# Transposing normalised rows with VectorE block turns and transfers through memory, in a planned transformer kernel on one core

## The chip, the core and the metric

The kernel runs on one core of a Trainium2 chip. The core has five engines with their own instruction queues: PE (TensorE, matrix products), DVE (VectorE), ACT (ScalarE), POOL (GpSimd) and SP (SyncE, which here issues nearly all DMA transfers). [...] The metric is the device time of the whole program in microseconds (us); lower is better.

## What is computed

Four attention blocks follow one another on a tensor of 8 batches x 256 rows x 128 features, all in float32. Block L2 is by far the largest: six layers, each with self-attention (16 heads of 64), cross-attention to 64 context rows, and a feed-forward part. Each of these three parts begins with a layer norm of its input. Cut to that:

```python
def _ln(x, g, b, eps=1e-05):
    m = jnp.mean(x, axis=-1, keepdims=True)
    v = jnp.mean(jnp.square(x - m), axis=-1, keepdims=True)
    return (x - m) / jnp.sqrt(v + eps) * g + b

def step(t, p):
    tn = _ln(t, norm_g, norm_b)
    t = _mha(tn, tn, skv, sq, sow, sob, tgt_mask) + t
    tn = _ln(t, norm_g, norm_b)
    t = _mha(src, tn, ckv, cq, cow, cob, src_mask) + t
    tn = _ln(t, pg, pb)
    t = t + (jax.nn.relu(tn @ w1 + b1) @ w2 + b2)
    return (t, None)
out, _ = jax.lax.scan(step, tgt, stacked)
```

Batches are independent of each other inside L2. L0 and L1 before it and L3 after it are single attention blocks.

## The kernel before

**Tiling.** One batch is 256 rows, kept as two tiles of 128 partitions by 128 features in `t`. [...] each normalised batch `xn` (rows on partitions) has to be turned into `tT` (128 features on partitions, 256 rows along the free dimension). There are 8 batches x 6 layers x 3 parts = 144 such turns.

**The helper `ahead`** (lines 764 to 816) makes each of them, in four steps with a place in the plan each: `moments` (L776, L777: mean and variance on DVE), `scales` (L782 to L789: reciprocal root and, for two of the three callers, minus mean times it, on POOL), `normal` (L795 on ACT for cross-attention and feed-forward, L800 on DVE for self-attention, writes `xn`) and `trans`. `trans` takes a PSUM tile, transposes the two 128x128 tiles of `xn` on PE against an identity (L809), and lets ACT copy the result to `tT` with the layer norm's gain and bias (L811).

**The plan.** The order of work is written by hand. `at(tick, phase, fn)` enters a function; at the end all functions are run in the order of tick, then phase, and every instruction of PE, DVE, ACT and POOL is tied behind the one before it on its engine. So the phase fixes the order on each engine inside a tick. SP is not among the tied engines.

- Self-attention of batch b at tick T = T0 + 4b: `exps` puts eight exponentials (L885) on ACT in each of ticks T to T+3, at phases 2 and 2.1, each preceded by a mask-and-minimum on DVE (L880). `scores` (L866) stand on PE at phases 1 and 1.1. The projections of the *next* batch run in the same ticks: k and q at T-4 and T-3 (L829, phases 3.5 to 3.7), v at T-2 and T-1 (L848). `values` (L921) and `out_proj` (L939) follow at phase 3 of later ticks.
- Cross-attention takes two ticks a batch: scores L341 and L348 on PE, then `lower` (copy L357 on ACT, maximum L359 on DVE, subtraction L360 on POOL), exponential L366 on ACT at phase 8, then sum L370, multiply L372 and turn L380 in the next ticks, and sums L388 on PE.
- Feed-forward takes one tick a batch: `first` (L1071 on PE, then ReLU L1076 on ACT) at T, `second` (L1088 on PE, added by L1092 on DVE) at T+1. Its last four ticks run together with the first projections of the next layer.

**Buffers and transfers.** PSUM has four two-bank tiles, shared by all products and transposes. Weights of a layer have one buffer each, and are loaded by SP in three functions `load_sa`, `load_ca` and `load_ff`, each issued at one place in the plan. SP also loads a mask of four transfers a batch (L246).

Of the kernel before, what the change touches and what calls it, by code (L numbers as in the profile page):

```python
# [8 lines left out]
F32 = mybir.dt.float32  # L9
I32 = mybir.dt.int32  # L10
BF16 = mybir.dt.bfloat16
AF = mybir.ActivationFunctionType
# [4 lines left out]
P = 128  # L17
B, S, D = 8, 256, 128
# [4 lines left out]
QT = S // P  # L23
# [4 lines left out]
def tile_xattn_stack(ctx: ExitStack, tc: tile.TileContext, io, out: bass.AP):  # L28
    nc = tc.nc
# [11 lines left out]
    def uniq(base):  # L41
        counter[0] += 1
        return f"{base}_{counter[0]}"
# [7 lines left out]
    def tp_tile():  # L51
        return one_bank("tp")
# [8 lines left out]
    def sb(shape, tag, bufs=2, pool=None):  # L61
        return (pool or act).tile(shape, F32, tag=tag, name=uniq(tag), bufs=bufs)
# [46 lines left out]
    ident = const.tile([P, P], F32, tag="ident", name="ident")  # L109
# [85 lines left out]
    def load_sa(l):  # L195
        sk = sb([D, H * HD], "w_sk", 1, wpool)
        nc.sync.dma_start(out=sk, in_=io["L2_sa_kv"][l][:, : H * HD])

        sv = sb([D, 4, 2, 2 * HD], "w_sv", 1, wpool)
        sv_v = io["L2_sa_kv"][l][:, H * HD :].rearrange("p (g a x) -> p a g x", g=2, a=4)  # L200
        for a in range(4):
            nc.sync.dma_start(out=sv[:, a], in_=sv_v[:, a])
        sq = sb([D, H * HD], "w_sq", 1, wpool)
        nc.sync.dma_start(out=sq, in_=io["L2_sa_q"][l])
        sow = sb([P, HC, D], "w_sow", 1, wpool)
        nc.sync.dma_start(out=sow, in_=io["L2_sa_ow"][l].rearrange("(c p) d -> p c d", p=P))
        ob = sb([P, D], "w_sob", 1, wpool)
        nc.sync.dma_start(out=ob, in_=io["L2_sa_ob"][l].partition_broadcast(P))
        W["sa", l] = (sk, sv, sq, sow, ob)

    def load_ca(l):

        ckv = sb([P, H * HD], "w_ckv", 1, wpool)
        for i in range(2):
            nc.sync.dma_start(
                out=ckv[DM * i : DM * i + DM],
                in_=io["L2_ca_kv"][l][:, H * HD * i : H * HD * (i + 1)],
            )
        cq = sb([D, H * HD], "w_cq", 1, wpool)
        nc.sync.dma_start(out=cq, in_=io["L2_ca_q"][l])  # L220
        cow = sb([P, HC, D], "w_cow", 1, wpool)
        nc.sync.dma_start(out=cow, in_=io["L2_ca_ow"][l].rearrange("(c p) d -> p c d", p=P))
        ob = sb([P, D], "w_cob", 1, wpool)
        nc.sync.dma_start(out=ob, in_=io["L2_ca_ob"][l].partition_broadcast(P))
        W["ca", l] = (ckv, cq, cow, ob)

    def load_ff(l):
        w1 = sb([D, FF], "w_f1", 1, wpool)
        nc.sync.dma_start(out=w1, in_=io["L2_ff_w1"][l])
        w2 = sb([P, FF // P, D], "w_f2", 1, wpool)  # L230
        nc.sync.dma_start(out=w2, in_=io["L2_ff_w2"][l].rearrange("(c p) d -> p c d", p=P))
        ob = sb([P, D], "w_fb", 1, wpool)
        nc.sync.dma_start(out=ob, in_=io["L2_ff_b2"][l].partition_broadcast(P))
        W["ff", l] = (w1, w2, ob)
# [44 lines left out]
    def at(tick, phase, fn):  # L279
        plan.setdefault(tick, []).append((phase, fn))  # L280
# [489 lines left out]
    def ahead(b, stats_at, normal_at, tT_at, g, bias, st, on_scalar=True):  # L770

        def moments():
            st["mv"] = sm([P, QT, 2], "mv")
            for j in range(QT):
                six = sm([P, 6], "six")
                nc.vector.bn_stats(six, tt(b)[:, j, :])  # L776
                nc.vector.bn_aggr(st["mv"][:, j, :], six)  # L777

        def scales():
            mv = st["mv"]  # L780
            ve = sm([P, QT], "ve")
            nc.gpsimd.tensor_scalar(ve, mv[:, :, 1], 1e-5, None, ALU.add)  # L782
            st["rstd"] = sm([P, QT], "rstd")
            nc.gpsimd.tensor_tensor(st["rstd"], ve, mhalf, ALU.pow)  # L784
            if on_scalar:
                nm = sm([P, QT], "nm")
                nc.gpsimd.tensor_tensor(nm, mv[:, :, 0], st["rstd"], ALU.mult)
                st["nm"] = sm([P, QT], "nm2")
                nc.gpsimd.tensor_scalar(st["nm"], nm, -1.0, None, ALU.mult)  # L789

        def normal():
            st["xn"] = sb([P, QT, D], "xn", 3)
            for j in range(QT):
                if on_scalar:
                    nc.scalar.activation(  # L795
                        st["xn"][:, j, :], tt(b)[:, j, :], AF.Identity,
                        scale=st["rstd"][:, j : j + 1], bias=st["nm"][:, j : j + 1],
                    )
                else:
                    nc.vector.tensor_scalar(  # L800
                        st["xn"][:, j, :], tt(b)[:, j, :], st["mv"][:, j, 0:1],
                        st["rstd"][:, j : j + 1], ALU.subtract, ALU.mult,
                    )

        def trans():
            ps = tp_tile()
            xn = st.pop("xn")
            for j in range(QT):
                nc.tensor.transpose(ps[:, j * P : (j + 1) * P], xn[:, j, :], ident)  # L809
            st["tT"] = sb([D, S], "tT", 3)  # L810
            nc.scalar.activation(st["tT"], ps[:, :S], AF.Identity, scale=g, bias=bias)  # L811

        at(*stats_at, moments)
        at(stats_at[0], 8.4, scales)
        at(*normal_at, normal)
        at(*tT_at, trans)

    def plan_sa(l, b, T):
# [134 lines left out]
        def mask():  # L953
            st["nm"] = load_mask(b)

        ahead(b, (T - 6, 8.3), (T - 5, 2.6), (T - 5, 7.2), norm_g, norm_b, st, False)
        at(T - 2, -1, mask)
        at(T - 4, 3.6, lambda: project(W["sa", l][2], "q", HD ** -0.5, 0, False))
        at(T - 4, 3.7, lambda: project(W["sa", l][2], "q", HD ** -0.5, 1, False))
# [58 lines left out]
    def plan_ca(l, b, T):  # L1018
        st = {}
        fold = W["fold", l]  # L1020

        def keys_both():

            res = [big("q", shape=(D, 4, 4, M)) for _ in range(2)]
            for g in range(2):
                ps = two_banks("mm").rearrange("p (r a x) -> p r a x", r=2, a=4)
                for a in range(4):
                    for r in range(2):
                        rows = slice(r * DM, (r + 1) * DM)
                        nc.tensor.matmul(  # L1030
                            ps[:, r, a, :], lhsT=fold["AT"][rows, 4 * g + a, :],
                            rhs=ctx2[rows, b : b + 2, :].rearrange("p b m -> p (b m)"),
                            start=True, stop=True,
                        )
                for i in range(2):
                    nc.scalar.copy(
                        res[i][:, :, 2 * g : 2 * g + 2, :].rearrange("p a r k -> p r a k"),
                        ps[:, :, :, i * M : (i + 1) * M],
                    )
            keys_of[b], keys_of[b + 1] = res  # L1040

        def make_values():
            st["VW"] = values_of(b, fold["WVO"])

        def res():
            st["tb"] = residual(b, W["ca", l][3])

        ahead(b, (T - 4, 6), (T - 3, 2.95), (T - 2, 2.9), norm_g, norm_b, st)
        if b % 2 == 0:
            at(T - 2, 3.7, keys_both)  # L1050
        at(T + 2, 3.2, make_values)
        at(T + 2, 7, res)

        def add(qt, ps):
            nc.vector.tensor_add(t[:, QT * b + qt, :], ps[:, :D], st["tb"][:, qt, :])

        for qt in range(QT):
            plan_weights_64(
                T + qt, qt, lambda: st["tT"], lambda: keys_of[b], lambda: st["VW"],
                nm2[:, b].unsqueeze(1).to_broadcast([P, 4, M]), lambda ps, qt=qt: add(qt, ps),  # L1060
            )

    def plan_ff(l, b, T):
        st = {}
# [28 lines left out]
                tt(b), ps[:, :S].rearrange("p (a d) -> p a d", a=QT), st["tb"]  # L1093
            )

        ahead(b, (T - 3, 6), (T - 2, 3.3), (T - 1, 2.9), pre_g[:, l : l + 1], pre_b[:, l : l + 1], st)
        at(T, 3.1, first)
        at(T + 1, 3.2, second)

# [61 lines left out]
            at(T + n, 4.5 - 0.1 * n, step)  # L1161


    at(0, -1, lambda: load_sa(0))
    at(8, -1, lambda: load_ca(0))
    at(8, -0.9, lambda: load_ff(0))
    plan_start()
    for b in range(B):
# [3 lines left out]
    for l in range(NL):  # L1172
        T_ca = T0 + 4 * B
        T_ff = T_ca + 2 * B
        for b in range(B):
            plan_sa(l, b, T0 + 4 * b)
        plan_ca_weights(l, T_ca - 6)
        for b in range(B):
            plan_ca(l, b, T_ca + 2 * b)
            plan_ff(l, b, T_ff + b)  # L1180
        if l > 0:
            at(T0, -1, lambda l=l: load_ff(l))
        if l + 1 < NL:
            at(T_ca + 4, -1, lambda l=l: load_sa(l + 1))
            at(T_ff + 1, -1, lambda l=l: load_ca(l + 1))
        T0 = T_ff + B
    def keys_l3():
        S0["k3T"] = sb([D, B, M], "AT", 1, heap)
# [3 lines left out]
    for b in range(B):  # L1192
# [1 line left out]

    engines = (
        mybir.EngineType.PE, mybir.EngineType.DVE, mybir.EngineType.Activation,
        mybir.EngineType.Pool,
    )
    order = mybir.DependencyInfo(mybir.DependencyClass.NoSync, mybir.DependencyReason.DATA)
    last = {}  # L1200
# [68 lines left out]
```

## Time and profile before

| | |
|---|---|
| median of 3 runs | 2530.57 us (2528.28 to 2533.17) |
| profiled execution, its own time | 2528.09 us |
| its span, first to last instruction | 2526.4 us |
| mean granted TensorE clock | 0.975 |
| busy: PEld (weight loads) | 1765.0 us, 70% |
| busy: DVE, ACT, POOL | 1822.0 (72%), 1735.1 (69%), 1443.0 us (57%) |
| the 288 transposes L809 on PE | 69.8 us busy, 307 ns each |
| the 144 copies L811 on ACT | 54.7 + 27.0 us busy, 570 and 563 ns each |
| DMA traffic | 64.31 MB, mean 25 GB/s |

A busy share is an average over stages. A layer takes about 380 us of the span; in the second one, for example, self-attention lies between about 570 and 800 us, cross-attention between about 800 and 900 us, and feed-forward, with the start of the next layer, up to about 957 us. PE's busy time is modelled from pipelined matmuls, so what PE costs is better read from the chain of waits and from the starts of instructions than from the busy share.

### The profile page before, as it was taken

To read this page: it belongs to the slowest core of one execution; us is meant where nothing else is said; L and a number is where in the kernel's file an instruction comes from. 1 tells how busy PE (TensorE), PEld (TensorE's weight loads), DVE (VectorE), ACT (ScalarE), POOL (GpSimd) and SP (SyncE) were. 2 spreads that over 40 slices of the span, in tenths; PEclk is the share of its full clock that TensorE was granted. 3 is DMA by queue.
4 is the path that set the end of the run, shared out by engine and by line. 5 is a ranking of instruction groups with operands and counts; after the bars stand their busy time and mean duration, and the time that the engine had idled before them with its cause. 6 is when DMAs were issued, how large, how long until landed. Compare 5 with 4: busy or idle time off the path is not lost.

```text
span 2526.4 us, 100196 instructions
## 1 busy us (share of the span) xinstructions
PE 2393.0 (95%) x42507; PEld 1765.0 (70%) x42507; DVE 1822.0 (72%) x5976; ACT 1735.1 (69%) x4537; POOL 1443.0 (57%) x2477
## 2 busy tenths in 40 slices
PE   6899999999999999999989999989999989999996
PEld 3566777776777776777776777776777776777774
DVE  3677887748887747887747887747887756888764
ACT  3467777657777657777657777657778657778651
POOL 2655556845556844555854555854555763555763
PEclk8999999999999999999999999999999999999996
DMA  5000012000002000002000102000012000000000
GB/s 161 11 2 20 19 35 64 2 8 24 20 28 65 8 7 24 20 20 70 12 2 21 28 20 70 12 2 20 20 28 70 12 2 20 20 20 12 3 1 17
DMA packets 94770, 64.31 MB, mean 25 GB/s; under 512 B 7729, under 2 KB 90353, under 8 KB 94322
## 3 DMA queue, kind: packets, MB, share of 16 engines
q1 hardware_dynamic: 93874, 57.64, 8.3%
q8 instruction: 334, 5.47, 0.9%
q14 instruction: 114, 0.93, 0.1%
q10 hardware_dynamic: 448, 0.26, 0.0%
HBM read 55.78 MB, written 2.10 MB: 23 GB/s over the span
## 4 chain that ended last, share of the span: by engine, by line
PE 69%; POOL 13%; DVE 8%; ACT 7%; issue 3%; DMA 0%; POOLq 0%; DVEq 0%; SPq 0%; ACTq 0%
PE mm L921 14%; PE mm L829 13%; PE sc L866 12%; PE mm L939 7%; PE mm L848 7%; POOL e L360 6%; PE mm L1071 3%; DVE m L359 3%; PE mm L1088 3%; POOL e L372 3%; ACT e L357 2%; PE mm L388 2%; ACT e L885 2%; PE sc L341 1%; POOL rstd L784 1%
## 5 line engine op out<-in xcount | busy, mean ns | idle before, releaser
L895 POOL TENSOR_SCALAR e<-e,rs 128x256 f32<-128x256 f32 x1536 | 702.5, 478 | 690.8 <-DVE rs L893 682.2
L885 ACT ACTIVATE e<-e,mn 128x256 f32<-128x256 f32 x1536 | 758.3, 495 | 131.0 <-DVE mn L880 130.2
L880 DVE CUSTOM_DVE_ANT_0 e<-sc,nm 128x256 f32<-128x256 f32 x1536 | 542.8, 419 | 122.5 <-PE sc L866 122.3
L905 DVE STREAM_TRANSPOSE eTc<-e 128x512 f32<-128x512 f32 x768 | 519.9, 697 | 66.2 <-POOL e L895 64.6
L921 PE MATMUL mm<-eTc,v 32*64 32x256 f32 x12288 | 381.2, 386 | 18.5 <-ACT AT L1007 8.1
L866 PE MATMUL sc<-k,q 64*32 64x256 f32 x12288 | 378.9, 380 | 5.9 <-DVE mn L880 4.2
L921 PEld LDWEIGHTS mm<-eTc,v 32*64 32x64 f32 x12288 | 284.1, 134 | 112.5 <-issue 27.7
L866 PEld LDWEIGHTS sc<-k,q 64*32 64x32 f32 x12288 | 220.2, 106 | 125.3 <-issue 45.8
L360 POOL TENSOR_TENSOR e<-e,m 128x1024 f32<-128x1024 f32 x112 | 213.1, 1903 | 148.6 <-DVE m L359 141.9
L885 ACT ACTIVATION_READ_ACCUMULATOR e<-e,mn 128x1 f32 x1536 | 286.7, 187 | 0.0
L359 DVE TENSOR_REDUCE m<-sc 128x16 f32<-128x1024 f32 x112 | 137.2, 1225 | 179.4 <-ACT e L357 179.4
L388 PE MATMUL mm<-v,k 128*128 128x128 f32 x1792 | 235.5, 287 | 5.9 <-DVE k L380 5.4
L388 PEld LDWEIGHTS mm<-v,k 128*128 128x128 f32 x1792 | 219.1, 200 | 27.4 <-issue 12.1
L341 PE MATMUL sc<-q,tT 128*32 128x256 f32 x3072 | 217.1, 382 | 0.0
L372 POOL TENSOR_TENSOR e<-e,r 128x1024 f32<-128x1024 f32 x112 | 213.2, 1904 | 0.7 <-DVE r L371 0.7
L366 ACT ACTIVATE e<-e 128x1024 f32<-128x1024 f32 x112 | 119.0, 1062 | 115.8 <-POOL e L360 115.8
L829 PE MATMUL mm<-tT,w_sk 128*128 128x256 f32 x768 | 189.6, 390 | 0.0
L286 ACT COPY v<-mm 128x1024 f32<-128x1024 f32 x96 | 97.2, 1012 | 133.1 <-PE mm L848 133.1
L939 PEld LDWEIGHTS mm<-w_sow,o 128*128 128x128 f32 x1536 | 175.1, 192 | 17.7 <-issue 14.4
L848 PE MATMUL mm<-w_sv,tT 128*32 128x256 f32 x3072 | 185.7, 382 | 0.0
L939 PE MATMUL mm<-w_sow,o 128*128 128x128 f32 x1536 | 183.6, 278 | 1.5 <-ACT WVO L1007 1.5
L829 PE MATMUL mm<-tT,w_sq 128*128 128x256 f32 x768 | 173.6, 379 | 0.0
(210 smaller groups left out, 3521.9 us busy)
## 6 DMA issues: line engine op xcount, KB each, us to landing
nm<-mask_d SPq DMA_DIRECT2D x192, 128.0 KB, 3.0
w_sk<-in_L_sa_kv_dram SPq DMA_DIRECT2D x6, 512.0 KB, 9.4
w_sv<-in_L_sa_kv_dram SPq DMA_DIRECT2D x24, 128.0 KB, 2.4
w_sq<-in_L_sa_q_dram SPq DMA_DIRECT2D x6, 512.0 KB, 3.5
w_sow<-in_L_sa_ow_dram SPq DMA_DIRECT2D x6, 512.0 KB, 4.0
w_ckv<-in_L_ca_kv_dram SPq DMA_DIRECT2D x12, 256.0 KB, 4.2
w_cq<-in_L_ca_q_dram SPq DMA_DIRECT2D x6, 512.0 KB, 4.6
w_cow<-in_L_ca_ow_dram SPq DMA_DIRECT2D x6, 512.0 KB, 4.0
```

The source lines that it names most:

```text
L360: nc.gpsimd.tensor_tensor(e, e, m.unsqueeze(2).to_broadcast([P, 16, M]), ALU.subtract)
L372: nc.gpsimd.tensor_tensor(tl["e"], tl["e"], r.unsqueeze(2).to_broadcast([P, 16, M]), ALU.mult)
L388: nc.tensor.matmul(ps[:, :D], lhsT=eT[:, s].rearrange("p q x -> p (q x)"), rhs=vw[:, r, k, g, :], start=(s == 0), stop=(s == 7),)
L829: nc.tensor.matmul(ps[:, i * S : (i + 1) * S], lhsT=w[:, c * P : (c + 1) * P], rhs=st["tT"], start=True, stop=True,)
L848: nc.tensor.matmul(ps[32 * a : 32 * a + 32, i, :], lhsT=st["tT"][:, kb * 32 : (kb + 1) * 32], rhs=sv[:, a].rearrange("p g x -> p (g x)"), ...
L866: nc.tensor.matmul(sc[32 * a : 32 * a + 32, r, j, :], lhsT=st["q"][g][rows, a, qb * 32 : (qb + 1) * 32], rhs=st["k"][g][rows, a, :], start ...
L880: nc.vector.tensor_tensor_reduce(e[:, i, :], sc4[:, i, :], st["nm"][:, 2 * jj + i % 2, :], -1.0, 3.0 * BIG, ALU.add, ALU.min, mn[:, i : i ...
L885: nc.scalar.activation(e[:, i, :], e[:, i, :], AF.Exp, scale=-1.0, bias=mn[:, i : i + 1], accum_out=rs[:, i : i + 1],)
L895: nc.gpsimd.tensor_scalar(e[:, i, :], e[:, i, :], rs[:, i : i + 1], 1.0, ALU.mult, ALU.mult)
L905: nc.vector.transpose(eT[:, r, :, 2 * jj : 2 * jj + 2, :], e[:, 2 * r : 2 * r + 2, :].rearrange("p j (k x) -> p k j x", x=32),)
L921: nc.tensor.matmul(ops[a // 2][r * HD : (r + 1) * HD, a % 2, :S], lhsT=st["v"][kb // 4][rows, kb % 4, (2 * g + r) * HD : (2 * g + r + 1) * ...
L939: nc.tensor.matmul(st["ps"][:, j * D : (j + 1) * D], lhsT=st["oT"][c // 4][:, c % 4, j * P : (j + 1) * P], rhs=sow[:, c, :], start=(c == 0 ...
```

## The change

`trans` no longer uses PE. A new step `blocks` turns each 32x32 block of `xn` on DVE into a tile `z`, and four transfers issued by SP write the blocks to a scratch tensor in memory, sorted by feature. A new step `fetch` reads them back with one transfer of 128 partitions x 1 KB into `raw`. `trans` then is only the ACT instruction with gain and bias, reading `raw` instead of PSUM. `trans` also moves to a later place in the plan for each of the three callers. SP joins the engines whose order is tied to the plan. The weight loads become generators, whose parts are entered in the plan one by one.

```diff
+        def blocks():
+            xn = st.pop("xn")
+            z = sb([P, 4, QT, 32], "z", 2)
+            nc.vector.transpose(z, xn.rearrange("p q (j x) -> p j q x", x=32))
+            zd = st["zd"] = dram.tile([4, 32, 4, QT * 32], F32, tag="zd", name=uniq("zd"), bufs=4)
+            for j in range(4):
+                nc.sync.dma_start(
+                    out=zd[j].rearrange("b i x -> i b x"), in_=z[:, j].rearrange("p q x -> p (q x)")
+                )
+
+        def fetch():
+            st["raw"] = sb([P, 4, QT, 32], "raw", 2)
+            nc.sync.dma_start(
+                out=st["raw"].rearrange("p i q x -> p (i q x)"),
+                in_=st.pop("zd").rearrange("j b i x -> (j b) (i x)"),
+            )
+
         def trans():
-            ps = tp_tile()
-            xn = st.pop("xn")
-            for j in range(QT):
-                nc.tensor.transpose(ps[:, j * P : (j + 1) * P], xn[:, j, :], ident)
             st["tT"] = sb([D, S], "tT", 3)
-            nc.scalar.activation(st["tT"], ps[:, :S], AF.Identity, scale=g, bias=bias)
+            nc.scalar.activation(
+                st["tT"].rearrange("p (q i x) -> p q i x", q=QT, i=4),
+                st.pop("raw").rearrange("p i q x -> p q i x"), AF.Identity, scale=g, bias=bias,
+            )
...
         at(*normal_at, normal)
+        at(normal_at[0], normal_at[1] + 0.01, blocks)
+        at(normal_at[0], 8.8, fetch)
         at(*tT_at, trans)
...
-        ahead(b, (T - 6, 8.3), (T - 5, 2.6), (T - 5, 7.2), norm_g, norm_b, st, False)
+        ahead(b, (T - 6, 8.3), (T - 5, 2.6), (T - 4, 2.15), norm_g, norm_b, st, False)
...
-        ahead(b, (T - 4, 6), (T - 3, 2.95), (T - 2, 2.9), norm_g, norm_b, st)
+        ahead(b, (T - 4, 6), (T - 3, 2.95), (T - 1, 2.15), norm_g, norm_b, st)
...
-        ahead(b, (T - 3, 6), (T - 2, 3.3), (T - 1, 2.9), pre_g[:, l : l + 1], pre_b[:, l : l + 1], st)
+        ahead(b, (T - 3, 6), (T - 2, 3.3), (T, 2.15), pre_g[:, l : l + 1], pre_b[:, l : l + 1], st)
...
-    at(0, -1, lambda: load_sa(0))
-    at(8, -1, lambda: load_ca(0))
+    def by_parts(tick, step, load, n):
+        for i in range(n):
+            at(tick + i * step, -1, lambda: next(load))
+
+    by_parts(0, 1, load_sa(0), 4)
+    by_parts(6, 1, load_ca(0), 3)
...
         if l > 0:
-            at(T0, -1, lambda l=l: load_ff(l))
+            at(T0 + 3, -1, lambda l=l: load_ff(l))
         if l + 1 < NL:
-            at(T_ca + 4, -1, lambda l=l: load_sa(l + 1))
-            at(T_ff + 1, -1, lambda l=l: load_ca(l + 1))
+            by_parts(T_ca + 4, 2, load_sa(l + 1), 4)
+            by_parts(T_ff + 1, 1, load_ca(l + 1), 3)
...
-        mybir.EngineType.Pool,
+        mybir.EngineType.Pool, mybir.EngineType.SP,
```

`load_sa` and `load_ca` get a `yield` after each weight (the last after the bias). The callers above are, in order, self-attention, cross-attention and feed-forward; in a call the three pairs are the places of `moments`, `normal` and `trans`.

More of the change, by code (lines that the diff above doesn't have):

```diff
@@ L197, in load_sa @@
         nc.sync.dma_start(out=sk, in_=io["L2_sa_kv"][l][:, : H * HD])
+        yield
         sv = sb([D, 4, 2, 2 * HD], "w_sv", 1, wpool)
@@ L202, in load_sa @@
             nc.sync.dma_start(out=sv[:, a], in_=sv_v[:, a])
+        yield
         sq = sb([D, H * HD], "w_sq", 1, wpool)
         nc.sync.dma_start(out=sq, in_=io["L2_sa_q"][l])
+        yield
         sow = sb([P, HC, D], "w_sow", 1, wpool)
@@ L209, in load_sa @@
         W["sa", l] = (sk, sv, sq, sow, ob)
+        yield
     def load_ca(l):
@@ L218, in load_ca @@
             )
+        yield
         cq = sb([D, H * HD], "w_cq", 1, wpool)
         nc.sync.dma_start(out=cq, in_=io["L2_ca_q"][l])
+        yield
         cow = sb([P, HC, D], "w_cow", 1, wpool)
@@ L225, in load_ca @@
         W["ca", l] = (ckv, cq, cow, ob)
+        yield
     def load_ff(l):
```

## The prediction

> **What bounds the kernel now.** I read the page first: busy shares, then the chain that ended last.
>
> ```profile
> PE 2393.0 (95%) x42507; PEld 1765.0 (70%) x42507; DVE 1822.0 (72%) x5976; ACT 1735.1 (69%) x4537; POOL 1443.0 (57%) x2477
> PE 69%; POOL 13%; DVE 8%; ACT 7%; issue 3%; DMA 0%; POOLq 0%; DVEq 0%; SPq 0%; ACTq 0%
> ```
>
> PE carries 69% of the chain, but not everywhere, so each stage has to be read alone. Self-attention first: the chain of waits over 690 to 800 us (start, length, what).
>
> ```profile
> 713.82 0.37 PE tp L809 x2
> 714.19 1.89 PE sc L866 x64
> 716.07 5.38 PE mm L829 x24
> 721.45 1.89 PE sc L866 x64
> ...
> 743.81 0.37 PE tp L809 x2
> ```
>
> Between these lines there is nothing but PE. A batch takes 29.99 us (743.81 - 713.82) and PE has no gap in it. The turn is worth 0.37 us of each batch. And tick T-4 (714.19 to 721.45) holds on PE only the scores of batch b-1 and the k and q projections of b: nothing else stands there that could fill a wait. The timeline of that tick shows where ACT is:
>
> ```profile
> 714.79 0.57 ACT L811 ACTIVATE tT<-tp,L_norm_b,L_norm_g 128x256 f32<-128x256 f32 x1
> ...
> 715.85 0.51 ACT L885 ACTIVATE e<-e,mn 128x256 f32<-128x256 f32 x1 [0.48 <-DVE mn L880]
> 716.00 1.99 PE L829 MATMUL mm<-tT,w_sk 128*128 128x256 f32 x8
> ...
> 719.30 0.49 ACT L885 ACTIVATE e<-e,mn 128x256 f32<-128x256 f32 x1
> 719.79 0.99 ACT L286 COPY k<-mm 128x1024 f32<-128x1024 f32 x1
> ```
>
> `tT` is written before the eight exponentials of the tick, and PE's projections start at 716.00, when ACT has only begun the first of them. The last ends at 719.79.
>
> Cross-attention, same chain view, around 860 to 872 us:
>
> ```profile
> 860.53 1.87 POOL e L360
> ...
> 863.39 1.00 ACT e L357
> 864.42 1.24 DVE m L359
> 865.73 1.90 POOL e L360
> 867.63 1.86 POOL e L372
> ...
> 871.85 1.88 POOL e L360
> ```
>
> Here a batch takes 11.32 us and no PE instruction is in it: POOL bounds it. Last, the windows (length, PE, PEld, DVE, ACT, POOL busy, granted clock, DMA share, GB/s): a batch of self-attention and the passage from cross-attention to feed-forward.
>
> ```profile
> 714.19:744.18 29.99, 29.99 (x650) 21.94 (x657) 25.36 (x98) 23.40 (x74) 16.17 (x36) 1.00 0.08 21
> 890.00:912.00 22.00, 17.10 (x124) 14.58 (x124) 11.90 (x32) 10.93 (x22) 13.79 (x20) 0.84 0.01 4
> ```
>
> The second shows what a pause of PE costs besides itself: the clock falls.
>
> [...] the clock records come in pieces of 3.41 us, at 1.0 or 0.5, and windows in which PE was active for less than about 0.38 are followed by one at half clock (894.27 to 897.69 after a pause from 891.8 to 894.4). [...] In the trace the output stores of 128 KB land after 1.8 us (median of the DMA view), so I use that; no run before shows 256-byte runs. [...]
>
> **The change part by part.**
>
> *PE loses 288 transposes.* 69.8 us busy, but 0.37 us a batch on the chain in self-attention, so 48 x 0.37 = 18 us there at most. In cross-attention nothing.
>
> *DVE gains 144 turns.* L905 takes 697 ns for 512 elements, so 0.37 us for 256 (0.33 to 0.7): 53 us busy. In self-attention it falls behind `normal` at tick T-5, where DVE waits 0.74 us for the scores afterwards (timeline, 715.32); in cross-attention DVE idles 1.41 and 2.12 us ahead of L359. Cost nothing; without that cover up to 0.37 each.
>
> *The trip through memory.* Mask loads issued one after the other start 0.49 us apart on SP (741.05, 741.55). Last store issued 1.5 us after the first, landed 1.8 later, then the fetch, 1.8: [...] 5.4 to 5.9 us from the turn to `raw`[...]. On SP the fetch waits for the stores, and mask and weight loads stand behind it; those are needed a tick or more later. Self-attention: turn ends near 712.9, lands near 718.6, and ACT reaches `trans` at 719.4 (below): hidden by 0.8 us. Cross-attention: turn ends at 851.9, lands at 857.6; the slot after L357 is at 858.3, and ACT idles from there to 860.57 (2.27 us before L795). Hidden by up to 3 us. DMA engines are at a share of 0.08 or less.
>
> *`trans` moves on ACT, self-attention.* From (T-5, 7.2) to (T-4, 2.15), which is behind `exps` at 2 and 2.1: behind all eight L885. The last of them ends 3.79 us after the first L829; I looked at all 48 batches: 3.79 in 34, 4.1 in two of the first layer, 1.84 to 2.19 in the second batch of each layer, and no exponential in the first batch's, which runs beside feed-forward. Then `trans` itself 0.57 (L811[...]) and 0.06 to PE (864.85 to 864.91). Scores and exponentials come 0.37 earlier together. So PE stands for 4.42 us with k, q, q, and everything later, behind it, and a batch grows by 3.79 + 0.57 + 0.06 - 0.37 = 4.05 us. 36 x 4.05 = 146, plus 6 x 2.1 = 13: **159 us**. Nothing can win it back: the rest of the period is PE alone.
>
> *Half clock after the stall.* [...] Averaged over the phase, PE then works about 2.8 us at half clock and loses 1.4 us: 36 x 1.4 = **50 us** (0 to 90).
>
> *Cross-attention.* `trans` goes from an even to an odd tick, into ACT's idle 2.27 us; the next scores need it later still. 0 (-6 to +10 in all).
>
> *Feed-forward and the next layer's start.* `trans` of the tick (2.15) now stands on ACT behind the copies of k, q, q, v of the tick before (phase 3.5 to 3.7), and `first` needs it at once. At 931.4 and 936.9 PE went from L829 straight on to L1071; now it waits for a copy of 1.02, `trans` 0.57, 0.06 = 1.65, less 0.22 to 0.37 for the turn: 1.4 x 3. In tick T_ff+3 two turns are due, so eight stores and two fetches pass SP: from 922.4, 3.5 us of issue, 1.8, 0.6, 1.8, then `trans` 0.57: projections start at 930.8 instead of 926.0, +4.8, and ReLU of the tick stands behind that `trans` on ACT. The two ticks before grow by some 0.8 each, since the trip (5.5) and ReLU, L795 and `trans` do not fit 4.5 and 4.8 us. Against this PE no longer waits for L795 at the end of cross-attention (2.61 us at 894.38). About 10 a layer, five layers: **50 us** (15 to 100).
>
> *Weight loads in parts, SP tied.* Each waits for a buffer whose last reader is done ticks before; 0. One PSUM tenant fewer: the one such wait that the list of waits shows on PE (L1030 for the PSUM that L811 reads) is 0.7 us at most, in a stage that POOL bounds; 0.
>
> **Sum.** 2528.1 (the profiled execution's own time, span 2526.4 and 1.7 around it) + 159 + 50 + 50 = 2787. The median is 2.5 above that execution: 2789; I say 2788 us.
>
> **Rivals.**
> 1. *The stall without the rest*: clock hardly falls, feed-forward costs 15. 2528 + 159 + 15 + 2 = 2704, say 2705. [...]
> 2. *Memory trip late*: 8.5 us instead of 5.7. Self-attention `raw` then lands 1.6 to 2 us after ACT gets there, +65; feed-forward +40. 2890. [...] Against: DMA is nearly idle.
> 3. *Not slower*: the projections find `tT` in time and the saving counts: 18 us in self-attention and some 15 from PE's waits for L795 (PE and PEld waited 89 us for it in all). 2530 - 33 = 2497. It needs ACT to finish `trans` within 0.37 us of the last scores' issue; the profile has the exponentials 3.79 us beyond, and ACT's order follows the phases (L811 always stood between L357 and L309 in cross-attention, as 2, 2.9, 3.2 say). Only if that order were not kept would it decide.
>
> **Numbers.** Forecast 0.6, rival 1 0.17, rival 2 0.17, rival 3 0.05, nothing either way 0.01. Range 2695 to 2880, with the unknown clock and feed-forward terms in it. A measurement here tells 0.2% (5 us) from no change. Faster 0.05, same 0.01, slower 0.94.
>
> **What would show it.** In the chain of self-attention: ACT L885 and `trans` ahead of L829, once in 34 to 36 us, and a wait of PE (or PEld) L829 for ACT tT of some 4.4 us, 36 times; half-clock records once a batch; cross-attention still 11.3 us a batch on POOL. If `trans` waits for the DMA of `raw` in self-attention, rival 2 is at work. If L829 follows the scores without a gap, I am wrong.

## The result and the profile after

The changed kernel takes 2874.03 us (median of 4 runs, 2867.36 to 2878.21), the kernel before 2531.87 us beside it: a ratio of 1.136, 95% interval 1.133 to 1.139. It is slower by 342 us. The forecast was 2788 us, range 2695 to 2880. Direction and mechanism came true; the loss was larger than forecast by a third, and the range held by only 6 us.

The profiled execution took 2877.27 us, span 2875.6. First the page: busy shares, and the chain by engine.

```profile
PE 2468.4 (86%) x42219; PEld 1816.3 (63%) x42219; DVE 1870.5 (65%) x6120; ACT 1750.7 (61%) x4537; POOL 1442.8 (50%) x2477
PE 39%; DVE 26%; ACT 13%; POOL 13%; issue 5%; DMA 3%; SPq 1%; DVEq 0%; ACTq 0%; POOLq 0%
```

PE lost 288 transposes and yet is busy for 75 us more, which suggests that something made its matmuls slower. And PE's share of the chain fell from 69% to 39%, with DVE and ACT in its place.

Where the time went I read by stage, from the starts of PE's instructions: self-attention from a layer's first scores to its last `out_proj` product, cross-attention from there to the first feed-forward product, feed-forward from there to the next layer's first scores. Sums over the six layers, in us:

| | before | after | difference | forecast |
|---|---|---|---|---|
| ahead of the first scores | 170.1 | 171.3 | +1.2 | 0 |
| self-attention | 1540.9 | 1804.1 | +263.2 | +209 |
| cross-attention | 477.0 | 479.1 | +2.1 | 0 |
| feed-forward | 303.9 | 386.9 | +83.0 | +50 |
| after the last feed-forward | 34.4 | 34.2 | -0.2 | 0 |

Now one tick T-4 of self-attention, in the timeline of the changed kernel (start, length, instruction; in brackets the idle time before it and what ended it). L893 are the scores, L912 the exponentials, L833 the ACT step of `trans`, L856 the projections, L820 and L826 the stores and the fetch.

```profile
768.06 2.18 SPq L820 DMA_DIRECT2D zd<-z  x4
768.69 1.96 PE L893 MATMUL sc<-k,q 64*32 64x256 f32 x64
...
770.41 0.51 ACT L912 ACTIVATE e<-e,mn 128x256 f32<-128x256 f32 x1 [0.58 <-DVE mn L907]
...
771.81 0.34 SPq L826 DMA_DIRECT2D raw<-zd  x1
...
773.87 0.49 ACT L912 ACTIVATE e<-e,mn 128x256 f32<-128x256 f32 x1
...
774.36 0.59 ACT L833 ACTIVATE tT<-raw,L_norm_b,L_norm_g 128x256 f32<-128x256 f32 x1
...
775.00 3.78 PE L856 MATMUL mm<-tT,w_sk 128*128 128x256 f32 x8 [4.35 <-ACT tT L833]
```

PE has its scores issued and then stands 4.35 us until `tT` is there. ACT is not waiting for the transfer: it goes from the last exponential to L833 without a gap. The fetch was issued at 771.81 and such fetches land after 2.07 us (median of the 144, worked out from the completion events), so `raw` was there at about 773.9, half a microsecond before ACT got to it. What makes PE wait is the order on ACT. The eight projections of k then take 3.78 us where before they took 1.99. The windows of two batches show that the clock was lower (length, PE, PEld, DVE, ACT, POOL busy, granted clock, DMA share, GB/s):

```profile
735.50:771.00 35.50, 31.11 (x640) 22.80 (x640) 25.77 (x101) 23.80 (x75) 16.23 (x35) 0.95 0.10 25
771.00:807.50 36.50, 32.14 (x640) 23.48 (x640) 25.75 (x101) 23.79 (x75) 16.24 (x35) 0.91 0.09 24
```

These two batches take 35.5 and 36.5 us in place of 30.0, and the clock in them is no longer 1.00. DVE's and ACT's work is the same as before to within half a microsecond.

In feed-forward the wait is another one. Tick T_ff+3 of the second layer, in which the third layer's first projections begin, same view (L1103 is the ReLU):

```profile
1025.51 4.46 SPq L820 DMA_DIRECT2D zd<-z  x8
...
1032.10 0.83 SPq L826 DMA_DIRECT2D raw<-zd  x2
1034.80 0.60 ACT L833 ACTIVATE tT<-raw,L_norm_b,L_norm_g 128x256 f32<-128x256 f32 x1 [8.06 <-DMA raw<-zd]
1035.30 1.54 ACT L1103 ACTIVATE o<-mm,L_ff_b1T 128x256 f32<-128x256 f32 x4
```

Eight stores and two fetches pass SP one behind the other, and ACT stands 8.06 us until the fetch has landed. The ReLU of the tick stands behind that step: its input was complete at 1028.78, and it starts at 1035.30.

### The profile page after: what moved, and what is told of

Its sections match the earlier page's. It is cut to its first block, busy times and chain, and to the rows that moved or that the text cites. A ratio compares the mean times of both kernels' runs of the same rounds, so it can differ in the third digit from the quotient of the medians.

```text
span 2875.6 us, 101045 instructions
## 1 busy us (share of the span) xinstructions
PE 2468.4 (86%) x42219; PEld 1816.3 (63%) x42219; DVE 1870.5 (65%) x6120; ACT 1750.7 (61%) x4537; POOL 1442.8 (50%) x2477
## 4 chain that ended last, share of the span: by engine, by line
PE 39%; DVE 26%; ACT 13%; POOL 13%; issue 5%; DMA 3%; SPq 1%; DVEq 0%; ACTq 0%; POOLq 0%
PE mm L856 15%; DVE e L907 8%; ACT e L912 7%; PE mm L948 6%; DVE eTc L932 6%; PE sc L893 5%; POOL e L367 5%; POOL e L922 4%; DVE m L366 3%; ACT e L364 3%; PE mm L1098 3%; PE mm L875 2%; POOL e L379 2%; ACT tT L833 1%; PE mm L1115 1%
## 5 line engine op out<-in xcount | busy, mean ns | idle before, releaser
L912 ACT ACTIVATE e<-e,mn 128x256 f32<-128x256 f32 x1536 | 758.2, 495 | 148.2 <-DVE mn L907 145.4
L856 PE MATMUL mm<-tT,w_sk 128*128 128x256 f32 x768 | 266.2, 506 | 205.8 <-ACT tT L833 205.8
L948 PE MATMUL mm<-eTc,v 32*64 32x256 f32 x12288 | 373.9, 381 | 21.8 <-DVE eTc L932 10.0
L893 PE MATMUL sc<-k,q 64*32 64x256 f32 x12288 | 379.2, 380 | 14.4 <-DVE o L291 8.6
L856 PEld LDWEIGHTS mm<-tT,w_sk 128*128 128x128 f32 x768 | 185.4, 254 | 273.4 <-ACT tT L833 225.2
L893 PEld LDWEIGHTS sc<-k,q 64*32 64x32 f32 x12288 | 220.1, 106 | 144.0 <-issue 59.8
L912 ACT ACTIVATION_READ_ACCUMULATOR e<-e,mn 128x1 f32 x1536 | 286.9, 187 | 0.0
L293 ACT COPY k<-mm 128x1024 f32<-128x1024 f32 x96 | 97.1, 1011 | 213.7 <-PE mm L856 213.7
L856 PE MATMUL mm<-tT,w_sq 128*128 128x256 f32 x768 | 198.6, 417 | 0.0
L856 PEld LDWEIGHTS mm<-tT,w_sq 128*128 128x128 f32 x768 | 169.1, 220 | 31.5
```

The lines of the kernel that those rows point to most:

```text
L856: nc.tensor.matmul(ps[:, i * S : (i + 1) * S], lhsT=w[:, c * P : (c + 1) * P], rhs=st["tT"], start=True, stop=True,)
L893: nc.tensor.matmul(sc[32 * a : 32 * a + 32, r, j, :], lhsT=st["q"][g][rows, a, qb * 32 : (qb + 1) * 32], rhs=st["k"][g][rows, a, :], start ...
L912: nc.scalar.activation(e[:, i, :], e[:, i, :], AF.Exp, scale=-1.0, bias=mn[:, i : i + 1], accum_out=rs[:, i : i + 1],)
L948: nc.tensor.matmul(ops[a // 2][r * HD : (r + 1) * HD, a % 2, :S], lhsT=st["v"][kb // 4][rows, kb % 4, (2 * g + r) * HD : (2 * g + r + 1) * ...
```

## The experiments

The theory: the place of `trans` on ACT, behind the eight exponentials, makes PE wait; the wait drops the clock; in feed-forward the same step stands behind copies and too near its own trip. The rival: the trip itself (DVE's turns, the transfers, SP's tied order) is what costs. Nine runs tell them apart; each ratio is to the kernel before, timed beside it on the same chip.

**1. Self-attention's place alone.** The changed kernel, with self-attention's layer norm one tick earlier and `trans` back ahead of the exponentials. The trip stays, and has one tick more time and four `raw` buffers in place of two.

```diff
-        ahead(b, (T - 6, 8.3), (T - 5, 2.6), (T - 4, 2.15), norm_g, norm_b, st, False)
+        ahead(b, (T - 7, 8.3), (T - 6, 2.6), (T - 5, 7.2), norm_g, norm_b, st, False)
...
-            st["raw"] = sb([P, 4, QT, 32], "raw", 2)
+            st["raw"] = sb([P, 4, QT, 32], "raw", 4)
```

> Changed kernel, self-attention alone moved: moments, normal and blocks one tick earlier, the ACT step of trans back at (T-5, 7.2), ahead of the eight exponentials; four raw buffers. Theory (the place of trans on ACT makes the stall): self-attention falls by about 263 us to that of before less 0.37 us a batch, in all 2874 - 263 - 18 = 2593 us (2560 to 2630), and PE goes from the scores to L856 without a gap. Rival (the trip through memory, DVE's turns or SP's tied queue slow self-attention): 2750 to 2880, with waits of ACT tT for the DMA of raw or of DVE behind z.

Measured: 2589.84 us, ratio 1.024 (1.022 to 1.026). The chain of waits in self-attention:

```profile
722.84 1.89 PE sc L893 x64
724.73 5.38 PE mm L856 x24
730.11 1.89 PE sc L893 x64
...
752.47 1.89 PE sc L893 x64
754.35 5.38 PE mm L856 x24
```

The projections follow the scores at once, at full speed, and a batch takes 29.63 us (752.47 - 722.84): 0.37 less than before, which is the turn that PE no longer makes. Self-attention is back at 1540.3 us with the trip still in it, so the 263 us lost in it go with the place of `trans`. It is not 13 us below the kernel before, though each steady batch is 0.37 us shorter: the first batches of a layer take longer (in the first layer 40.2 us from the first batch's scores to the second's, against 38.2). Feed-forward keeps 365.6 us.

**2. The place without the trip.** The kernel before, PE turns and all, with self-attention's `trans` moved to (T-4, 2.15).

```diff
-        ahead(b, (T - 6, 8.3), (T - 5, 2.6), (T - 5, 7.2), norm_g, norm_b, st, False)
+        ahead(b, (T - 6, 8.3), (T - 5, 2.6), (T - 4, 2.15), norm_g, norm_b, st, False)
```

> Kernel before, PE turns kept, no transfers and no DVE turn; only self-attention's trans moved from (T-5, 7.2) to (T-4, 2.15). Theory: the same stall of PE L829 for ACT tT of 4.4 us and the same fall of the clock, 36 x (4.05 + 0.37 + 2.3) plus some 20 for the second batches: 2532 + 262 = 2790 us (2740 to 2820). Rival (the trip is the cause): 2532 us.

Measured: 2776.57 us, ratio 1.098 (1.096 to 1.100). In its chain (L885 the exponentials, L811 `trans`, L829 the projections):

```profile
713.73 1.33 ACT e L885 x5
715.06 0.06 issue
715.13 2.64 ACT e L885 x11
717.77 0.46 ACT tT L811
718.23 0.04 issue
718.27 8.49 PE mm L829 x24
726.76 1.89 PE sc L866 x64
```

Not one transfer or DVE turn was added, and 247 us are lost, with the same exponentials and `trans` on the chain and the same slow projections (8.49 us in this batch). Self-attention takes 1791.0 us, 250 more than before. That leaves the rival 13 of the 263 us there.

**3. The trip without the place.** Turns, stores and fetches of the changed kernel on top of PE turns at their old places; the fetched tile is read by nobody. SP tied and weights in parts as in the changed kernel.

```diff
         def blocks():
-            xn = st.pop("xn")
+            xn = st["xn"]
...
         def trans():
-            st["tT"] = sb([D, S], "tT", 3)
-            nc.scalar.activation(
-                st["tT"].rearrange("p (q i x) -> p q i x", q=QT, i=4),
-                st.pop("raw").rearrange("p i q x -> p q i x"), AF.Identity, scale=g, bias=bias,
-            )
+            ps = tp_tile()
+            xn = st.pop("xn")
+            for j in range(QT):
+                nc.tensor.transpose(ps[:, j * P : (j + 1) * P], xn[:, j, :], ident)
+            st["tT"] = sb([D, S], "tT", 3)
+            nc.scalar.activation(st["tT"], ps[:, :S], AF.Identity, scale=g, bias=bias)
```

> PE turns and places of the kernel before, and on top of them the DVE turns, the stores and the fetches of the changed kernel, whose result is read by nobody; SP tied and weights loaded in parts as in the changed kernel. It does added work and computes the same output by the old way. Theory: all this is hidden, 2532 us (2527 to 2545). Rival (DVE, DMA or SP carry the loss): 2600 us or more.

Measured: 2543.62 us, ratio 1.005 (1.004 to 1.007). The added work is not quite free: 14.6 us, 4% of the whole loss. By the stage reckoning above, self-attention takes 11.8 and feed-forward 5.8 us more, cross-attention 3.1 less. In the middle of self-attention the chain shows PE alone and batches of 30.0 us, as before. About half of the 11.8 lies in the first two batches of a layer, where DVE is on the chain (in the second layer with a turn of 0.45 us), the rest behind the last batch's first scores.

**4. SP's order alone.** The kernel before with SP tied and the weight loads in parts, that is, run 3 without its turns and transfers.

```diff
-        at(normal_at[0], normal_at[1] + 0.01, blocks)
-        at(normal_at[0], 8.8, fetch)
```

> Kernel before with SP tied to the plan and the weights loaded in parts, nothing else of the change. My forecast costs this at nothing: 2529 us (2524 to 2534). If e3_trip_only's 14 us came from SP's order, 2540 or more; if part of e8's gain comes from it, 2515 to 2523.

Measured: 2527.07 us, ratio 0.9993 (0.998 to 1.000). No difference; this part of the change costs nothing, and run 3's 14.6 us belong to turns and transfers. Which of the two was not tried.

**5. The clock, first try.** To keep PE active in the wait, 18 products of weights with weights ahead of the first projection, into the tile that the projection overwrites.

```diff
+            if tag == "k" and c4 == 0 and b >= 2:
+                for i in range(18):
+                    nc.tensor.matmul(
+                        ps[:, :S], lhsT=w[:, :P], rhs=w[:, S : 2 * S], start=True, stop=True,
+                    )
             for i in range(4):
```

> Changed kernel with 18 products of weights with weights on PE ahead of the first projection of batches 2 to 7 (3.9 us, inside the stall of 4.4 us; their result is overwritten). Theory: the stall stays, but PE stays active, so the half-clock windows after it go: 36 x 2.3 = 83 us less, 2790 us (2770 to 2815), L856 x24 back at 5.1 us. Rival (the longer projections come from something else than the clock, or the clock costs only the 1.4 us of my forecast): 2874 or 2824 us.

Measured: 2903.27 us, a miss, ratio 1.148 (1.145 to 1.151). The chain says what was wrong with the experiment (L856 is now the filling, L861 the projections):

```profile
743.38 1.89 PE sc L898 x64
745.27 7.97 PE mm L856 x36
753.24 5.18 PE mm L861 x24
```

Each of these products left two matmul records of 0.22 us. 18 products took 7.97 us and outlasted the wait. Yet the 24 projection records after it take 5.18 us.

**6. The clock, with the right size.** The same with `range(9)`, 3.9 us.

> As e4_warm_pe with 9 products in place of 18. Each is two matmul records of 0.22 us, so 18 had taken 7.97 us and outlasted the stall of 4.4; 9 take 3.9 us. Theory (half clock after the stall): PE stays at full clock, the 24 projection records take 5.2 us in place of 7.4, 36 x 2.2 = 80 us less than the changed kernel: 2795 us (2775 to 2815). Rival: 2824 (clock costs my 1.4 us) or 2874 (no clock effect).

Measured: 2796.51 us, ratio 1.105 (1.103 to 1.107), 77.5 us under the changed kernel. The wait is still there, and the projections are back:

```profile
754.02 1.33 ACT e L917 x5
755.42 2.64 ACT e L917 x11
758.06 0.50 ACT tT L833
758.61 5.45 PE mm L861 x24
764.05 1.89 PE sc L898 x64
```

The window of this batch has the full clock:

```profile
754.02:788.08 34.06, 33.79 (x669) 25.09 (x658) 25.74 (x99) 23.77 (x74) 16.33 (x36) 1.00 0.11 26
```

In batches 3 to 8 of every layer the time from the first to the last of the 24 projection records is 5.07 us, as in the kernel before; in the changed kernel it is 7.37 us on average (6.4 to 8.1). A batch takes 34.06 us, 4.43 more than in run 1, which is the wait alone. The clock records agree: none at half clock touches the pause or the projections of these 36 batches here, in the kernel before or in run 1, and all 36 are touched in the changed kernel. So the 2.3 us a batch go with the half clock.

**7. Feed-forward's place too.** On top of run 1:

```diff
-        ahead(b, (T - 3, 6), (T - 2, 3.3), (T, 2.15), pre_g[:, l : l + 1], pre_b[:, l : l + 1], st)
+        ahead(b, (T - 4, 6), (T - 3, 3.3), (T - 1, 2.9), pre_g[:, l : l + 1], pre_b[:, l : l + 1], st)
```

> As e1_sa_early, and feed-forward moved too: moments and normal one tick earlier, (T-4, 6) and (T-3, 3.3), and the ACT step of trans back at (T-1, 2.9). Theory (what is left of the loss in e1 is trans behind the copies and too near its trip in feed-forward, 366 us over six layers against 304): feed-forward back to 304 to 320 us, in all 2590 - 50 = 2540 us (2515 to 2555). Rival (the trips themselves, DVE and SP work, carry it): 2575 to 2590.

Measured: 2542.95 us, ratio 1.005 (1.004 to 1.006). Feed-forward is at 310.7 us, cross-attention at 485.5. Of the 342 us lost, 13 are left, with the trip still in all 144 places. That is near run 3's 14.6, but it lies elsewhere: 8.5 us in cross-attention and 6.8 in feed-forward, while self-attention, with its steady batches shorter and its first ones longer, is 1.2 above the kernel before. Where the 8.5 come from was not tried.

**8. The trip only where PE bounds.** Run 1's self-attention; cross-attention and feed-forward turn on PE at the places of before.

```diff
+        if on_scalar:
+            at(*tT_at, turn_on_pe)
+        else:
+            at(normal_at[0], normal_at[1] + 0.01, blocks)
+            at(normal_at[0], 8.8, fetch)
+            at(*tT_at, trans)
```

> The trip through memory in self-attention alone, one tick early as in e1_sa_early; PE turns at the places of before in cross-attention and feed-forward. Theory: self-attention keeps the 0.37 us a batch, 36 x 0.37 = 13 us, and nothing else is lost: 2516 us (2508 to 2526), faster than both kernels. Rival (the trip's own work costs as much as in e3_trip_only): 2529 us or more.

Measured: 2508.24 us (2506.11 to 2510.05), ratio 0.991 (0.990 to 0.993): faster than both kernels. Self-attention takes 1533.4 us, cross-attention 470.3, feed-forward 300.5. A batch in the chain of waits, 29.63 us from scores to scores:

```profile
713.96 1.89 PE sc L904 x64
715.85 5.38 PE mm L867 x24
...
743.59 1.89 PE sc L904 x64
```

**9. Its control.** Run 8's earlier layer norm, but with PE turns.

```diff
-        ahead(b, (T - 6, 8.3), (T - 5, 2.6), (T - 5, 7.2), norm_g, norm_b, st, False)
+        ahead(b, (T - 7, 8.3), (T - 6, 2.6), (T - 5, 7.2), norm_g, norm_b, st, False)
```

> Kernel before with self-attention's moments and normal one tick earlier, PE turns and trans at their old places: the schedule of e8_trip_in_sa_only without the trip. If the gain of e8 (21 us) is PE's 0.37 us a batch, this is no faster than before: 2529 us (2522 to 2536). If it comes from the earlier layer norm, 2508 to 2515.

Measured: 2529.06 us, ratio 1.000 (0.999 to 1.001). The earlier layer norm alone gives nothing, and SP's order (run 4) gives nothing, so run 8's gain comes with the turn that PE is spared. But it is not all the turn's own time. The 36 x 0.37 are 13 us, and since the first batches of a layer take longer, the stage reckoning shows 7.5 in self-attention. Cross-attention gives 6.7 and feed-forward 3.4, though their code is that of the kernel before. For cross-attention the clock records say with what this goes: the stage takes 78.3 to 78.4 us in every layer in which none of it is at half clock (all six in run 8, one in the kernel before, two in run 9), and 79.4 to 80.1 in the other layers of these kernels. The kernel before also varies with its clock, from 2522.21 us at a mean of 0.978 to 2534.42 at 0.972. Against that quickest execution, timed on another chip, run 8 with its 0.978 to 0.979 is 14 us ahead. Why run 8's cross-attention stays at full clock, and whether by luck, was not tried.

## Why the prediction was right, and where its sizes were off

**The bound, and the wait that takes its place.** Right. That self-attention is PE without a gap, that nothing else stands in tick T-4, and that `trans` falls behind eight exponentials, gave the pause of 4.42 us. Measured from the last scores' instruction to the first projection, most batches show 4.73 us against 0.31 before, so 4.42 more; the mean over batches 3 to 8 is 4.64 more. In five of these batches `trans` did wait for its fetch (0.23 to 0.93 us, 2.7 in all). Less the 0.37 saved, 36 x 4.27 = 154 us, forecast 146. The second batches lost 6.1 us in the first layer and 2.5 in the others, 16 us net, forecast 13. Runs 1 and 2 show both directions. With the 83 us of the next paragraph these make 253 of the 263. The trip's own work (11.8 us in run 3) and half clock in three of the second batches (6 us) are together more than the 10 left, so the terms do not quite add up.

**Half clock: the mis-sized term.** The step's estimate, worked out from the 4.42 us pause, the 3.41 us of the clock records and the 0.38 read off the kernel before, said that PE works about 2.8 us at half clock after a pause and loses 1.4, 50 us in all. Measured, and shown by run 6, are 2.3 us a batch: 36 x 2.3 = 83 us, inside the stated 0 to 90 but off by 33 us. What was missing is in the clock records. In both kernels every record but the last is a whole multiple of 3.41 us long; a window here is one such piece, and its activity the share of it that matmul records cover. In the kernel before, all 8 full-clock windows under 0.38 were followed by half clock (in the one from 890.86 to 894.27 PE is busy for 0.91 us, and the next is at 0.50), but so were 14 of the 691 above, so 0.38 was not shown to be a limit. The estimate also let a half-clock window end after 3.41 us unless it too was idle for over 2.1 us. The counts of the changed kernel say otherwise. Its windows at full clock were followed by half clock 55 times of 55 when their activity was under 0.4, 10 of 89 between 0.4 and 0.8, and 1 of 575 above. Its windows already at half clock were followed by another 49 times of 49 under 0.8, 3 of 8 between 0.8 and 0.9, and 3 of 63 at 0.9 and more, all three after 2800 us. So a pause that ended inside a half-clock window could cost that window's rest and the whole next one: in the 36 steady batches half clock lasted one window in 10 and two in 26, and after the pause PE spent 4.7 us in it on average, against 2.8 forecast. A second estimate of mine, from these counts (half clock left at an activity of 0.85) and the same 4.42 us pause, averaged over where it falls in the windows, gives 4.4.

**Feed-forward: right in kind, 83 us in place of 50.** The double trip was forecast to let the projections start 4.8 us later; PE waits 4.88 us ahead of the third layer's (4.2 to 5.3 in the five). PE's L1098 waits for `tT` 34 times, 51.1 us in all. The three waits a layer that were forecast at 1.4 are there, at 1.60 to 1.63 us in layers 1 to 5. The two ticks that were to grow by 0.8 each have waits of 2.6 to 3.3 us and of 0 to 2.3: too small a term. Two terms were left out: half clock after the pauses, which makes the first batch's 24 projections 6.75 to 7.59 us long against 4.97 (11 us in all), and the sixth layer, to which I gave nothing and which lost 13.0 us.

**What was costed at nothing.** Cross-attention: +2.1 us over six layers, right. SP tied and weights in parts: right (run 4). The trip hidden in self-attention: right but for the 2.7 us above; in the tick shown it has 0.5 us to spare where 0.8 was forecast, and takes 5.8 us from the turn's end, forecast 5.4 to 5.9. The turn takes 435 ns and not 0.37 us, stores follow each other after 0.56 us, and the fetch is issued 2.15 us after the last store. Turns and transfers at nothing: wrong by 14.6 us (run 3), which lie at the edges of the stages; in the steady batches of that run no loss shows.

**The rivals.** The clock did fall (a mean of 0.929 against 0.975 before), so rival 1 is out; the trip was late in self-attention only in the five batches above, so rival 2, which wanted 65 us there, is out (its 8.5 us for the trip was an estimate that no run shows; the tick shown has 5.8), though in feed-forward its mechanism was part of the forecast itself. Rival 3 would have needed `trans` ahead of the exponentials: run 1 is that case for self-attention.

## What to carry to other kernels

Here, moving an operation off the engine that bounds a stage paid what the chain showed for it (0.37 us a batch), and the place where its result is now made was worth more than the operation. So ask what stands ahead of it on the new engine, and who waits with nothing else to do. Give a trip through memory its own whole tick ahead, and use it only in the stage that the relieved engine bounds. On PE, price a pause with its clock: here 4.4 us of waiting brought 2.3 us of slower work behind it.

## What the runs showed of the hardware that was not expected

- In the changed kernel all 49 half-clock windows with a PE activity under 0.8 were followed by another at half clock, and 3 of the 63 with 0.9 and more. Half clock followed all 55 full-clock windows under 0.4 and 11 of the 664 above.
- The same wait without the fall of the clock was had by giving PE work that nobody reads: 9 products a batch made the changed kernel 77.5 us faster.
- The stores have runs of 256 bytes, 32 KB each. The fetch, which waits for them, was issued 2.15 us after the last of four (median), and its 128 KB landed after 2.07 us. No run has longer runs to compare.
- ACT took 594 ns to read `raw` from SBUF in pieces of 32 elements, where it had taken 570 from PSUM in one piece. Source and pieces changed together.
